# A two-layer decoder kernel: the retention's tiles placed at both ends of the on-chip memory, the experts' weights loaded inside the retention stage, and the last groups' routing written out

## The chip, the cores and the metric

The kernel runs on one core of one Trainium2 chip, as one launch. Its time is the device time in microseconds (us). A change is judged by the median of several runs: before the change, twelve runs gave a median of 1694.53 us, from 1690.32 to 1700.62. One core has a matrix engine (PE, with PEld for loading its stationary operand), a vector engine (DVE), a scalar engine (ACT), a general engine (POOL) and an engine that here only issues transfers (SP). Each takes its own instructions in order and waits on semaphores for the others.

## The reference, cut to what matters

The input x has 32 sequences of 128 tokens with 256 channels, in float32, and there is a context of the same shape. Six sublayers follow one another, each of the form x = x + f(layernorm(x), ...): in layer 0 an attention, a retention against the context, and a mixture of eight experts; in layer 1 another attention-like sublayer, a cross attention, and another mixture of experts. The change touches the border between the second and the third:

```python
def _L0_xattn_ref(query, key, value, W_Q, W_K, W_V, g_w, g_b, out_w, out_b):   # retention
    q, k, v = (einsum('bld,hde->bhle', ...) for query, key, value)             # 16 heads of 16
    q, k = _xpos(q, downscale=False), _xpos(k, downscale=True)
    sim = einsum('bhnd,bhsd->bhns', q, k) * _decay_mask(L, H)[None]
    ret = einsum('bhns,bhsd->bhnd', sim, v)
    ret = (ret - mean(ret)) / sqrt(var(ret) + GN_EPS)                          # per head
    gate = silu(query @ g_w.T + g_b)
    return ret * gate @ out_w.T + out_b

def _L0_ffn_ref(x, Wg, W1, W2, W3):                # 8 experts, D = 256, H = 512, the best 2
    top_vals, top_idx = top_k(x @ Wg, 2)
    weights = softmax(top_vals), placed at top_idx
    return sum over e of weights[e] * ((silu(x @ W1[e]) * (x @ W2[e])) @ W3[e])
```

## The kernel before, in words

**Stages.** `sublayers` calls the stages in order: `stage_a` (first attention), `stage_b` (retention), `stage_c` (the experts of layer 0), then the stages of layer 1. x stays in the on-chip memory all the time, in eight groups of GB = 4 sequences. The pools of a stage are opened when it begins and given back when it ends, so a later stage's tiles lie where an earlier stage's were, and the first write to such a tile waits for the last reader of what lay there.

**Retention.** `stage_b` loops `for b in range(B + 8)` over the 32 sequences, as a pipeline of steps written out by hand. In pass b the sequence b+2 is projected, b+1 is turned and scored, b is multiplied with its values (`values`, matmuls at L897) and normed per head (`norm`: variance on DVE, L915, inverse root on POOL, L149, product and bias on POOL), b-2 is gated (`gated`: transposes at L928, product on DVE at L930, tile b_oT) and b-3 gets its output projection (`out`: matmuls at L935, sum into x on DVE at L939). The last eight passes only drain this pipeline. The order on PE is the written one (`manual_schedule`); the instructions of DVE, ACT and POOL are ordered by the compiler's scheduler, which a hint (`order`, here as the argument `behind`) can tie to come after a given instruction.

**Routing.** When the four sequences of a group have left the retention, the group is routed to the experts, in five steps one pass apart, from pass 4g+7 on: `start` (statistics of the layer norm on DVE, L175, whose inverse root ln_rs is one POOL instruction at L149), `norm` (four DVE instructions at L203 write the normed tokens into the tile c_h), `turn` (transposes at L241, copies by ACT and DVE at L244 and L246 into c_hT), `choose` (router matmuls at L158; some twenty small DVE instructions at L320 to L341 find the best two experts, the last of them giving r_both; they also write two columns of c_h), and `place` (matmuls at L356 and L357 count the tokens ahead; DVE works out the rows r_rowi). From pass 4g+11 on, `store` writes one sequence's c_h into the table r_xs in device memory, by two indirect scatters that POOL issues (L344), one for each of the two experts chosen: eight scatters a group. Only the last group's stores stand behind the loop. The tile c_h has two buffers, so group g's norm may write only when group g-2's scatters have read theirs.

**Experts.** `stage_c` opens a pool for the experts' weights, the tile c_wx, of 12.6 MB, and loads it on SP with one transfer of 1.5 MB for each expert (L1007). Its place is where the retention's tiles lay. Then come small loads for later (`load_late`, L106), and `finish` works out where each expert's tokens begin. The table is read in 71 blocks of 128 tokens (L443, tile c_xb), each by a plain transfer on SP that must follow all scatters. On PE a block takes two transposes (L1026), eight matmuls into the two hidden halves (L1034), four transposes (L1047) and eight matmuls out (L1054); the weights are addressed by an expert number in a register, read for twelve blocks at a time. The result leaves by an indirect scatter (L344).

Of the kernel before, what the change touches and what calls it, by code (L numbers as in the profile page):

```python
# [22 lines left out]
F32 = mybir.dt.float32  # L23
# [5 lines left out]
P = 128  # L29
B = 32  # L30
# [11 lines left out]

NX = 2 * NC * FF0 + NF0 * D
# [18 lines left out]
WB = dict(q=(0, 256), k=(256, 256), v=(512, 272), kr=(784, 128), g=(912, 256), o=(1168, 256))  # L62
N_WB = 1424


class K:
# [51 lines left out]
    def load_late(self, pool):  # L118

        self.const = pool  # L120
        self.rows2 = self.load("rows2", [1, N_ROWS - N_ROWS1])
        self.wE = self.load("wE", [P, NC, 2 * D])
        self.wr1 = self.load("wr1", [P, NC, E])
        self.sw1 = self.load("sw1", [P, NC, P])
        self.sw2 = self.load("sw2", [P, D])
        self.rb2 = self.load("rb2", [P, D])
        self.eb = self.load("eb", [P, E])
# [20 lines left out]
    def rsqrt(self, out, in_, n):  # L148
        self.nc.gpsimd.tensor_tensor(out, in_, self.mhalf[: in_.shape[0], 0:n], ALU.pow)  # L149
# [344 lines left out]
class Route:  # L494
# [11 lines left out]
    def norm(self, behind=None):  # L506
        self.h = self.tile([P, GB, W["r"]], "h", bufs=2)
        self.k.normed(self.g, self.h, self.stats, behind)

    def turn(self):  # L510
        self.hT = self.tile([P, NC, GT], "hT")
        self.k.transposed(self.hT, self.h)
# [232 lines left out]
def load_b(k, p1):  # L745

    for name, key, shape in (
        ("wB", "wB", [P, NC, N_WB]), ("trig", "trig", [P, 2, 2 * D]), ("decay", "decay", [P, 4, 4, P]),
        ("ob", "outb", [P, D]),
    ):  # L750
        t = p1.tile(shape, F32, name=f"b_{name}")
        k.nc.sync.dma_start(out=t, in_=k.ins[key])
        setattr(k, name, t)


def stage_b(k, p1):
# [6 lines left out]
    with (  # L763
        tc.tile_pool(name="b2", bufs=2) as p2,
        tc.tile_pool(name="b3", bufs=3) as p3,
        tc.tile_pool(name="c2", bufs=1) as pc,
    ):
        trig, decay, ob = k.trig, k.decay, k.ob
# [19 lines left out]
        class Group:  # L788
            def __init__(self, g):
# [11 lines left out]
                self.gate = p2.tile([P, NC, GB, P], F32, name="b_gate")  # L801
# [26 lines left out]
        class Seq:  # L828
# [63 lines left out]
            def values(self):  # L892
# [9 lines left out]
                self.rT = p2.tile([P, NC, P], F32, name="b_rT")  # L902
                nc.scalar.copy(self.rT, pr)

            def norm(self):
# [3 lines left out]
                self.ret = p3.tile([P, H, HD], F32, name="b_ret")  # L909
                nc.scalar.copy(self.ret, pt.rearrange("p (h d) -> p h d", d=HD))  # L910
                sq = p2.tile([P, H, HD], F32, name="b_sq")
                nc.scalar.activation(sq, self.ret, AF.Square)
                var = p2.tile([P, H], F32, name="b_var")
                nc.vector.tensor_reduce(var, sq, AX.X, ALU.add)
                nc.vector.tensor_scalar(var, var, 1.0 / HD, GN_EPS, ALU.mult, ALU.add)  # L915
                rs = p2.tile([P, H], F32, name="b_rs")
# [7 lines left out]
            def gated(self):  # L924
# [4 lines left out]
                self.oT = p2.tile([P, NC, P], F32, name="b_oT")  # L929
                self.gated_by = nc.vector.tensor_mul(self.oT, pt, self.group.gate[:, :, self.i, :]).ins  # L930

            def out(self):
                po = k.bank([P, D])
                for c in range(NC):
                    nc.tensor.matmul(  # L935
                        po, lhsT=self.oT[:, c, :], rhs=k.wb("o", c), start=c == 0, stop=c == NC - 1
                    )
# [3 lines left out]
        with tc.manual_schedule(engines={mybir.EngineType.PE}):  # L941
# [19 lines left out]
            for b in range(B + 8):  # L961
# [31 lines left out]
                if 0 <= lag < NG - 1:  # L993
                    routes[lag].store(rest, seqs[b].last if b < B else None)
            for rest in range(GB):
                routes[NG - 1].store(rest)


def stage_c(k, later):
    nc, tc = k.nc, k.tc  # L1000
    with (
        tc.tile_pool(name="c1", bufs=1) as p1,
        tc.tile_pool(name="c3", bufs=3) as p3,
    ):
        wx = p1.tile([P, E, NX], F32, name="c_wx")
        for e in range(E):
            nc.sync.dma_start(out=wx[:, e, :], in_=k.ins["wx"][e])  # L1007
        later()
# [3 lines left out]
        def weights(j, o, n):  # L1012
            return wx[:, bass.ds(d.regs[j][0], 1), o : o + n].rearrange("p n f -> p (n f)")

        class Block:
# [15 lines left out]
            def up(self, u):  # L1031
                pu = k.bank([P, FF0], "s")
                for c in range(NC):
                    nc.tensor.matmul(  # L1034
                        pu, lhsT=self.xT[:, c, :], rhs=weights(self.j, (2 * c + u) * FF0, FF0),
# [15 lines left out]
            def down(self):  # L1051
                py = k.bank([P, D])
                for f in range(NF0):
                    nc.tensor.matmul(  # L1054
                        py, lhsT=self.hid[:, f, :], rhs=weights(self.j, 2 * NC * FF0 + f * D, D),
# [715 lines left out]
def sublayers(ctx, k):  # L1771
# [4 lines left out]
    with tc.tile_pool(name="b1", bufs=1) as pb:  # L1776
        def later():
            load_b(k, pb)
            k.empty = p1.tile([P, W["r"]], F32, name="r_empty")
            k.nc.vector.memset(k.empty, 0.0)  # L1780
            k.nc.vector.memset(k.empty[:, D : D + 2], -1.0)
            k.table("r", B, pd)
            k.deal = Deal(k, p1)
            k.disp = Dispatch(k, "r", 0, B, p1, p2)
            for n, name in enumerate(("g0", "g1")):
                k.table(name, B // 2, pd)
            for e in range(E):
                k.clear("r", e)

        stage_a(k, later)  # L1790
        stage_b(k, pb)
    late = pool("late")
    stage_c(k, lambda: k.load_late(late))
# [44 lines left out]
def layout(inputs):  # L1838
# [16 lines left out]
    def spread(w):  # L1855
# [27 lines left out]
            rep_w.reshape(D, P), a["L0_xattn_g_w"].T, a["L0_xattn_out_w"].T,  # L1883
        ], axis=1)),
        outb=np.broadcast_to(a["L0_xattn_out_b"], (P, D)),
        wg0=chunks(a["L0_ffn_Wg"]),
        wx=np.concatenate([
            w12.reshape(E, 2, NC, P, FF0).transpose(0, 3, 2, 1, 4).reshape(E, P, -1),
            a["L0_ffn_W3"].reshape(E, NF0, P, D).transpose(0, 2, 1, 3).reshape(E, P, -1),
        ], axis=2),  # L1890
# [36 lines left out]
```

## Time and profile before

| what | value |
|---|---|
| median of 12 runs | 1694.53 us |
| profiled execution | 1700.53 us |
| its span, from first to last instruction | 1698.4 us |
| mean PE clock granted | 0.921 |
| busy time: PE, PEld | 1488.4 (88%), 986.1 (58%) |
| busy time: DVE, ACT, POOL | 930.1 (55%), 606.1 (36%), 602.0 (35%) |
| r_xs scatters of L344 on POOL | 64, in all 64.3 us |
| ln_rs of L149 on POOL | 40, in all 40.7 us, 1022 ns each |
| c_wx loads | 8, of 1536 KB each |
| chain by engine | PE 69%, DVE 12%, POOL 5%, issue 5%, ACT 5%, DMA 3% |

By stretch, from a table of windows (us of the span; busy us of PE, DVE and POOL; granted clock; DMA share):

| window | what runs | PE | DVE | POOL | clock | DMA |
|---|---|---|---|---|---|---|
| 282 to 540 | most of the retention | 241.07 | 189.80 | 183.70 | 0.99 | 0.26 |
| 540 to 604 | its end, routing of groups 5 to 7, load of the weights | 22.62 | 30.99 | 37.43 | 0.59 | 0.69 |
| 604 to 1024 | the experts of layer 0 | 417.40 | 141.72 | 68.33 | 0.99 | 0.15 |

How to read such a profile: a busy share is a mean over stages with different limits, so a stage is read by itself. A row of a timeline gives the start, the length, the engine, the line, the operation, the tiles written and read, their shapes, and in square brackets how long the engine stood idle before it and what released it. A chain of waits goes back from an instruction to whatever released it, step by step; where a DMA stands in it, its length is the time from issue to landing. "issue" means that nothing the profile shows was waited for. An idle engine costs time only where the chain passes through it.

### The profile page before, as it was taken

Reading aid. Unit: us, or ns where it says so; the run is one execution under the profiler, and the core shown is the slowest. Engines: PE = TensorE matmul, PEld = TensorE weight load, DVE = VectorE, ACT = ScalarE, POOL = GpSimd, SP = SyncE. Lnnn points to the kernel's source line nnn. Section 1 sums busy time; section 2 is a strip of 40 time slices with the busy share of each in tenths; the row PEclk is TensorE's granted clock in tenths of the full one; section 3 lists DMA queues with packets and bytes.
Section 4 is the critical chain, followed back from the end, with each engine's and each line's share of the span. In section 5 each row is a group of like instructions: output and inputs, shape, how many; then the busy total and the mean of one; then the engine's idle time right before and its main releaser. Section 6 shows DMA issues by size and latency. Waiting matters only on the chain.

```text
span 1698.4 us, 26941 instructions
## 1 busy us (share of the span) xinstructions
PE 1488.4 (88%) x9233; PEld 986.1 (58%) x9233; DVE 930.1 (55%) x3005; ACT 606.1 (36%) x1542; POOL 602.0 (35%) x621
## 2 busy tenths in 40 slices
PE   6999799999998379999999994789999998878882
PEld 4555567776776346666666664445555554456672
DVE  6666446777778533333333324546567766554565
ACT  2444333433333022222222221155665554433341
POOL 2111136577768511111111113121233433365553
PEclk8999999999999589999999995799999998778997
DMA  9990199711000821111111108000000110043486
GB/s 337 336 336 18 54 326 318 228 39 36 24 26 33 349 95 49 44 45 48 47 45 44 50 23 314 13 6 6 3 2 14 53 55 26 26 128 110 131 269 228
DMA packets 133113, 183.85 MB, mean 108 GB/s; under 512 B 12043, under 2 KB 113237, under 8 KB 130933
## 3 DMA queue, kind: packets, MB, share of 16 engines
q1 hardware_dynamic: 116356, 142.28, 26.8%
q0 software_dynamic: 13296, 36.52, 6.0%
q10 hardware_dynamic: 3328, 3.33, 0.6%
q8 instruction: 77, 1.26, 0.3%
q14 instruction: 56, 0.45, 0.1%
HBM read 69.80 MB, written 112.30 MB: 107 GB/s over the span
## 4 chain that ended last, share of the span: by engine, by line
PE 69%; DVE 12%; POOL 5%; issue 5%; ACT 5%; DMA 3%; another core or an unknown queue 1%; POOLq 0%; ACTq 0%; SPq 0%; DVEq 0%
PE ps L1034 13%; PE ps L1054 6%; PE ps L158 5%; PE ps L666 3%; PE ps L1458 3%; PE ps L1418 2%; PE ps L1436 2%; PE ps L1642 2%; PE ps L1658 2%; PE ps L241 2%; PE ps L881 2%; PE ps L1047 2%; PE ps L153 2%; PE ps L897 1%; PE ps L840 1%
## 5 line engine op out<-in xcount | busy, mean ns | idle before, releaser
L1034 PE MATMUL ps<-c_wx,c_xT 128*128 x568 | 268.8, 596 | 0.0
L344 POOL DMA_INDIRECT r_ys<-c_yb,r_toi x71 | 67.9, 956 | 356.0 <-DVE r_w L462 315.7
L1034 PEld LDWEIGHTS ps<-c_wx,c_xT 128*128 128x128 f32 x568 | 103.2, 192 | 73.8 <-issue 70.3
L1054 PE MATMUL ps<-c_wx,c_hid 128*128 x568 | 134.8, 380 | 0.9 <-DVE c_hid L1049 0.9
L1054 PEld LDWEIGHTS ps<-c_wx,c_hid 128*128 128x128 f32 x568 | 107.4, 190 | 47.2 <-issue 17.9
L887 DVE TENSOR_TENSOR b_sim<-ps,b_decay 128x512 f32<-128x512 f32 x128 | 79.5, 682 | 84.5 <-PE ps L881 51.2
L149 POOL TENSOR_TENSOR b_rs<-b_var,mhalf 128x16 f32<-128x16 f32 x32 | 93.6, 2927 | 82.8 <-DVE b_var L915 79.7
L1059 ACT ACTIVATE c_yb<-ps,r_w 128x256 f32<-128x256 f32 x71 | 33.7, 474 | 219.2 <-PE ps L1054 219.2
L1049 DVE COPY c_hid<-ps 128x512 f32<-128x512 f32 x71 | 49.1, 691 | 101.2 <-PE ps L1047 101.2
L344 POOL DMA_INDIRECT g_ys<-f_yb,g_toi x78 | 75.6, 969 | 66.2 <-DVE g_to L449 49.7
L1443 DVE TENSOR_REDUCE e_pad<-ps 128x4 f32<-128x512 f32 x128 | 82.3, 681 | 13.7 <-PE ps L1436 8.9
L149 POOL TENSOR_TENSOR ln_rs<-ln_ve,mhalf 128x4 f32<-128x4 f32 x40 | 40.7, 1022 | 132.2 <-DVE ln_ve L177 132.1
L1488 POOL TENSOR_TENSOR x<-x,e_t 128x256 f32<-128x256 f32 x32 | 23.3, 727 | 163.2 <-DVE e_t L1483 163.2
L175 DVE BATCH_NORM_STATS2 ln_st<-x 128x6 f32<-128x256 f32 x192 | 74.9, 406 | 9.8 <-DMA x<-in_x_dram 5.1
L1042 DVE TENSOR_TENSOR c_su<-ps,c_su 128x512 f32<-128x512 f32 x71 | 49.1, 691 | 56.0 <-PE ps L1034 56.0
L1459 ACT ACTIVATE e_e<-ps 128x512 f32<-128x512 f32 x128 | 67.5, 605 | 28.4 <-PE ps L1458 28.2
L344 POOL DMA_INDIRECT r_xs<-c_h,r_rowi x64 | 64.3, 1004 | 28.7 <-issue 14.8
L1040 ACT ACTIVATE c_su<-ps 128x512 f32<-128x512 f32 x71 | 42.4, 597 | 86.8 <-PE ps L1034 86.8
L344 POOL DMA_INDIRECT g_xs<-f_h,g_rowi x64 | 63.2, 987 | 24.7 <-issue 15.9
L1436 PE MATMUL ps<-kp,e_qT 32*128 32x128 f32 x1024 | 67.0, 308 | 1.6 <-ACT e_e L1459 1.0
L1658 PE MATMUL ps<-f_rw,f_hb 128*128 x156 | 51.6, 415 | 15.6 <-ACT f_hb L1654 12.0
L1642 PE MATMUL ps<-f_rw,f_xT 128*128 x312 | 53.6, 299 | 11.9 <-ACT f_xT L1634 8.5
(385 smaller groups left out, 3325.2 us busy)
## 6 DMA issues: line engine op xcount, KB each, us to landing
g_xs<-r_empty SPq DMA_DIRECT2D x16, 2193.0 KB
r_xs<-r_empty SPq DMA_DIRECT2D x8, 4290.0 KB
c_wx<-in_wx_dram SPq DMA_DIRECT2D x8, 1536.0 KB
f_xb<-g_xs SPq DMA_DIRECT2D x78, 129.0 KB
c_xb<-r_xs SPq DMA_DIRECT2D x71, 130.0 KB
c_yg<-r_ys SPq DMA_DIRECT2D x8, 1024.0 KB
f_yg<-g_ys SPq DMA_DIRECT2D x16, 512.0 KB
x<-in_x_dram SPq DMA_DIRECT2D x8, 512.0 KB
```

What stands on the lines that cost most here:

```text
L149: self.nc.gpsimd.tensor_tensor(out, in_, self.mhalf[: in_.shape[0], 0:n], ALU.pow)
L158: self.nc.tensor.matmul(out, lhsT=(xT[c] if isinstance(xT, tuple) else xT[:, c])[:, i * P : (i + 1) * P], rhs=w(c), start=c == 0, stop=c = ...
L175: self.order(nc.vector.bn_stats(st[:, i, :], x[:, i, :]).ins, behind)
L344: inst = self.nc.gpsimd.indirect_dma_start(out=table, out_offset=bass.IndirectOffsetOnAxis(ap=rows, axis=0), in_=src, in_offset=None,).ins
L887: nc.vector.tensor_mul(self.sim[:, r].rearrange("p c s t -> p (c s t)"), ps[r].rearrange("p c s t -> p (c s t)"), decay[:, r].rearrange("p ...
L1034: nc.tensor.matmul(pu, lhsT=self.xT[:, c, :], rhs=weights(self.j, (2 * c + u) * FF0, FF0), start=c == 0, stop=c == NC - 1,)
L1054: nc.tensor.matmul(py, lhsT=self.hid[:, f, :], rhs=weights(self.j, 2 * NC * FF0 + f * D, D), start=f == 0, stop=f == NF0 - 1,)
L1436: nc.tensor.matmul(ps[r][:, j, :], lhsT=self.group.qT[rows, j, self.i, :], rhs=self.keys[rows, :], start=True, stop=True,)
L1443: nc.vector.tensor_reduce(slots[:, :, r, HD], ps[r], AX.X, ALU.max, negate=True)
L1459: self.exp_by = nc.scalar.activation(self.e[:, r], ps, AF.Exp, scale=1.0 / 16.0).ins
L1642: nc.tensor.matmul(pu, lhsT=self.xT[:, c, :], rhs=experts.rw1[:, self.at, c, :].rearrange("p n f -> p (n f)"), start=c == 0, stop=c == NC - 1,
L1658: nc.tensor.matmul(po, lhsT=self.hid, rhs=experts.rw2[:, self.at, :].rearrange("p n f -> p (n f)"), start=True, stop=True,)
```

## The change

The computation is the same; five things differ.

1. *Pools.* The pools of the retention that are still needed after the last `values` (b3, now with the tiles b_gate, b_rT, b_sq, b_var, b_rs, b_ret and b_oT, and c2 with the routing's tiles) lie at the right end of the memory. The output projection's weights leave the common weight tile and become a tile of their own, `wo`, in a pool bl at the right end too, with a load of their own. The pools b1 (projection weights, tables, padded values) and b2 stay at the left and are given back inside the stage, after the loop.
2. *The loop* ends at `range(B)`. Then b2 and b1 are closed and `over()` loads the experts' weights: so the load stands, on SP, ahead of the last steps, and it waits for the last readers of what lay there. After it the last steps are written out one by one: the last `gated` and `out`, and the routing of groups 5, 6 and 7. Group 6's norm has no `behind`; group 6's stores are tied behind the inverse root of group 7's layer norm (`last = k.rooted`).
3. *Buffers.* c_h has three buffers for two; c_hT comes out of the pool and the buffers of the layer norms' h.
4. *The experts' weights* are eight tiles for one: four of [128, 8, 512] for the hidden halves (2 MB each) and four of [128, 8, 256] for the output (1 MB each), loaded by eight transfers; the arrays passed to the kernel are laid out accordingly.
5. *The late loads* go to a pool at the right end.

```diff
@@ rsqrt
-        self.nc.gpsimd.tensor_tensor(out, in_, self.mhalf[: in_.shape[0], 0:n], ALU.pow)
+        inst = self.nc.gpsimd.tensor_tensor(out, in_, self.mhalf[: in_.shape[0], 0:n], ALU.pow)
+        self.rooted = inst.ins
@@ class Route
-        self.h = self.tile([P, GB, W["r"]], "h", bufs=2)
+        self.h = self.tile([P, GB, W["r"]], "h", bufs=3)
...
-        self.hT = self.tile([P, NC, GT], "hT")
+        self.hT = self.k.lnp.tile([P, NC, GT], F32, name="c_hT", tag="h")
@@ load_b
+def load_b(k, p1, last):
+    for pool, name, key, shape in (
+        (p1, "wB", "wB", [P, NC, N_WB]), (p1, "trig", "trig", [P, 2, 2 * D]), (p1, "decay", "decay", [P, 4, 4, P]),
+        (last, "wo", "wo", [P, NC, D]), (last, "ob", "outb", [P, D]),
     ):
@@ stage_b
-        tc.tile_pool(name="b2", bufs=2) as p2,
-        tc.tile_pool(name="b3", bufs=3) as p3,
-        tc.tile_pool(name="c2", bufs=1) as pc,
+        tc.tile_pool(name="b3", bufs=2, side="right") as p3,
+        tc.tile_pool(name="c2", bufs=1, side="right") as pc,
+        ExitStack() as most,
     ):
+        p2 = most.enter_context(tc.tile_pool(name="b2", bufs=2))
...
-                        po, lhsT=self.oT[:, c, :], rhs=k.wb("o", c), start=c == 0, stop=c == NC - 1
+                        po, lhsT=self.oT[:, c, :], rhs=k.wo[:, c, :], start=c == 0, stop=c == NC - 1
...
-            for b in range(B + 8):
+            for b in range(B):
...
-                if 0 <= lag < NG - 1:
-                    routes[lag].store(rest, seqs[b].last if b < B else None)
+                if 0 <= lag:
+                    routes[lag].store(rest, seqs[b].last)
+            most.close()
+            over()
+
+            r5, r6 = routes[NG - 3], routes[NG - 2]
+            step("gated", B - 2)
+            step("out", B - 3)
+            r6.norm()
+            for rest in range(1, GB):
+                r5.store(rest)
+            step("out", B - 2)
+            r6.turn()
+            step("gated", B - 1)
+            r6.choose()
+            step("out", B - 1)
+            r7 = RouteC(k, NG - 1, k.disp, pc)
+            last = k.rooted
+            r7.norm()
+            r6.place()
             for rest in range(GB):
-                routes[NG - 1].store(rest)
+                r6.store(rest, last)
+            r7.turn()
+            r7.choose()
+            r7.place()
+            for rest in range(GB):
+                r7.store(rest)
@@ experts
+class Glu:
+    def load(self, pool):
+        tile = lambda name, n: pool.tile([P, E, n], F32, name=f"c_{name}")
+        self.up = [tile(f"up{i}", FF0) for i in range(2 * NC)]
+        self.down = [tile(f"down{i}", D) for i in range(NF0)]
+        for tiles, name in ((self.up, "wxu"), (self.down, "wxd")):
+            for i, t in enumerate(tiles):
+                self.k.nc.sync.dma_start(out=t, in_=self.k.ins[name][i])
...
-        wx = p1.tile([P, E, NX], F32, name="c_wx")
-        for e in range(E):
-            nc.sync.dma_start(out=wx[:, e, :], in_=k.ins["wx"][e])
-        later()
+        k.load_late()
...
-        def weights(j, o, n):
-            return wx[:, bass.ds(d.regs[j][0], 1), o : o + n].rearrange("p n f -> p (n f)")
+        def weights(j, tile):
+            return tile[:, bass.ds(d.regs[j][0], 1), :].rearrange("p n f -> p (n f)")
@@ sublayers
+    last, most, weights = (ctx.enter_context(ExitStack()) for _ in range(3))
+    pb = most.enter_context(tc.tile_pool(name="b1", bufs=1))
+    pl = last.enter_context(tc.tile_pool(name="bl", bufs=1, side="right"))
+    glu = Glu(k)
...
+    def over():
+
+        most.close()
+        glu.load(weights.enter_context(tc.tile_pool(name="c1", bufs=1)))
+
+    stage_a(k, later)
+    stage_b(k, pb, pl, over)
+    last.close()
+    k.const = pool("late", side="right")
+    stage_c(k, glu)
+    weights.close()
```

## The prediction

> **What bounds the kernel now.** I read, in this order, the page's slices (PE falls to 3 tenths in the fourteenth slice, 552 to 594 us, while DMA stands at 8), then a table of ten-microsecond windows around that slice, the chain of waits through it, the DMA queue's own waits, and POOL's timeline. The kernel is PE-bound on both sides of the slice (PE 9 tenths or more), so what counts is the stretch from the last retention matmul to the first expert matmul.
>
> The windows (busy us of PE, PEld, DVE, ACT, POOL; PE clock; DMA share; GB/s):
>
> ```profile
> 540.00:550.00 10.00, 6.07 (x63) 5.23 (x63) 8.05 (x39) 2.65 (x5) 8.58 (x8) 0.89 0.16 55
> 550.00:560.00 10.00, 7.88 (x36) 6.44 (x34) 4.76 (x18) 0.59 (x1) 8.53 (x8) 0.60 0.15 50
> 560.00:570.00 10.00, 0.43 (x4) 0.33 (x3) 2.51 (x18) 0.21 (x1) 4.39 (x5) 0.57 0.98 387
> 590.00:600.00 10.00, 0.00 (x0) 0.00 (x0) 3.68 (x10) 0.00 (x0) 6.31 (x7) 0.50 0.98 386
> ```
>
> PE does almost nothing from 560 to 604 us, the DMA engines are full from 560 to 600, and PE's clock sinks to 0.5. It looks as if the weights' load were the wait. The chain says otherwise (start, us, what):
>
> ```profile
> 563.29 8.34 DMA r_xs<-c_h,r_rowi
> 571.76 0.41 DVE c_h L203
> ...
> 597.18 4.40 DMA r_xs<-c_h,r_rowi
> 601.78 0.35 SPq L443
> 602.32 2.32 DMA c_xb<-r_xs
> ```
>
> The reader is to see that two landings of routing scatters carry it: the last scatter of group 5 lands 8.34 us after its issue and only then may the norm of group 7 overwrite that buffer; and the last scatter of group 7 lands at 601.58, after which the first block is read and PE starts at 603.95. The load of the weights itself (line 1007) is seen in the queue's waits:
>
> ```profile
> SPq L1007 <- DVE b_oT L930: 169.9, 1, 169.9
> SPq L1007 <- PE ps L935: 4.0, 1, 4.0
> SPq L106 <- DMA c_wx<-in_wx_dram: 22.5, 6, 4.6
> ```
>
> It is issued at 558.87, when the last L935 is done. The small loads behind it (L106) each wait for one weight load; the seventh is done at 592.59, and at 22.5 / 6, some 4 us each, the eighth at about 597. That is 4.6 us before the scatter's 601.58: the load is not the last wait, though it slows those that are. POOL's queue in between:
>
> ```profile
> 541.81 2.94 POOL L149 TENSOR_TENSOR b_rs<-b_var,mhalf 128x16 f32<-128x16 f32 x1 [0.70 <-DVE b_var L915]
> ...
> 546.34 1.06 POOL L344 DMA_INDIRECT r_xs<-c_h,r_rowi  x1 [0.17 <-issue]
> 547.70 0.96 POOL L344 DMA_INDIRECT r_xs<-c_h,r_rowi  x1 [0.30 <-issue]
> 548.68 1.04 POOL L149 TENSOR_TENSOR ln_rs<-ln_ve,mhalf 128x4 f32<-128x4 f32 x1
> ...
> 554.33 1.06 POOL L344 DMA_INDIRECT r_xs<-c_h,r_rowi  x1 [0.17 <-issue]
> ...
> 563.29 0.96 POOL L344 DMA_INDIRECT r_xs<-c_h,r_rowi  x1 [0.30 <-issue]
> 564.26 1.05 POOL L149 TENSOR_TENSOR ln_rs<-ln_ve,mhalf 128x4 f32<-128x4 f32 x1
> ```
>
> A group's eight scatters take 554.33 to 564.25, 1.27 us each, and group 6's ln_rs, at 548.68, stands behind two of them.
>
> **The change, part by part.** The order of the built kernels shows the same instructions on PE, DVE, ACT and POOL, moved only in the tail, and one DMA more on SP. Times below are on the clock of the profiled execution.
>
> *The load moves.* Its first DMA now waits for the last L897, which ends at 541.54 + 1.08 = 542.62, not for L935 at 558.74: 16.1 us earlier, at about 542.75. The old load took from 558.87 to 597, 38 us; so it ends near 581. Alone this gains nothing on the chain, since a scatter was 4.6 us later than it; it takes the load away from the end, where the scatters of group 7 land. With busy DMA the last landing took 4.40; at the end of the expert stage, with idle DMA, the same kind of scatter took 2.95 (1023.56 to 1026.51). I take 2.95: minus 1.45.
>
> *Third buffer for c_h.* Group 7's norm now waits for scatters issued at 546.34 and 547.70, long landed, not for the one at 563.29. In the old run ln_rs was ready at 565.31 and the norm began at 571.76: 6.45 us of wait go. What is late next is ln_rs itself.
>
> *The new order on DVE.* This costs. Without its ordering hint, the norm of group 6 (L203) now stands right behind r_m of 544.15, ahead of the var of the last sequence and of all of group 5's choosing. It needs ln_rs, which POOL ends at 549.72 as before. So DVE stands still from 544.33 to 549.8. Behind it: PE's place matmuls (L356) of group 5, behind them on PE the last gated and out steps; b_var for POOL's last b_rs. From 549.8 I add pitches of the old timeline (0.33 for each 256-wide operation, 0.1 to 0.2 for each small one): four L203, var, two L939 and L175, and the small ones make 3.75, so r_both is issued at 553.55 where it was 547.72; L356 at 553.85 (548.07), L357 ends near 555.1, r_at 555.15, and the rows, behind b_oT, at 556.7 (550.8). Group 5's eight scatters run from 556.85, not 554.33: 2.5 later, to 566.75. One thing can lengthen this: L915 took 0.70 beside a POOL operation and 0.16 without; a small DVE operation caught so beside POOL's b_ret and x (0.62 + 0.72) costs up to 1.4. I take none, and keep 1.4.
>
> *PE meanwhile.* Idle since 544.64, it resumes at half clock: L928 0.67 and L935 1.91 to 557.65, as at 549.03. In the old run four microseconds of work brought the full clock back (L241 1.91 from 555.72, then L158 x16 in 1.85 from 558.58). So from 557.9: L935 to 558.9, L241 x8 1.04 to 559.9, c_hT 0.7, L158 1.85 to 562.5, L935 1.03 to 563.5; then DVE's choose steps and the last statistics to about 565.2. That is before POOL is free at 566.75, so POOL decides: ln_rs to 567.8, the norm of group 7 at 567.85. It was 571.76: minus 3.9.
>
> *From there* to the next matmul (L241, 574.85 before) the old run took 3.09; in the new order r_both stands before the third L203, and I count 2.75: minus 0.35. Then nothing differs up to POOL's first scatter of group 7 (587.84 before), and PE is again at half clock, having idled 5 us (2.6 us sufficed at 531.7). Sum at that point 4.25 earlier, 583.6; group 6's scatters, from 571.8, are out by 581.7. The last scatter follows 8.9 later (7 x 1.27; 9.34 before): minus 0.45. Then the landing, minus 1.45, and 2.37 as before to PE.
>
> *The sum:* -3.9 -0.35 -0.45 -1.45 = -6.15; I round to -6.0. The profiled execution took 1700.53 (span 1698.4 and 2.1 around it), 6.0 above the median of the runs, 1694.53. It would take 1694.5, and the median 1688.5.
>
> *At nothing:* the weights as eight tiles of 2 and 1 MB for eight of 1.5 MB (same bytes; in the expert stage each block takes PE 5.82 us with no gap, so addresses are computed under it); the output weights as a load of their own (one issue, 0.43 on SP, behind it table clears whose queue then waits 90.8 us for DVE; without that cover 0.43); c_hT in the norms' buffers; the late loads, now free after the last L935 and done well before 590.
>
> *A rule against it.* The Trainium skill, "DMA: Bandwidth & Descriptors", section "Queues, rings and completion order", has each DMA engine go round its queues and empty a whole packet of one before the next. In the trace four scatters issued from 559.50 to 563.29 had landed by 571.63, with the load in flight from 560.9: 2.7 each, faster than one per weight load of 4.4. By the rule, with larger tiles, one scatter per load, estimated at 5.9 us for a 2 MB tile and 3 for a 1 MB one: group 5's eighth lands at 581.5 and holds back group 6's eighth, which waits for it. The sum would be -5.3. By the trace's 2.7 it lands at 578.5, before that scatter's turn at 580.7, and the sum stays.
>
> **The rivals.**
> *Half clock to the end of the retention (chance 0.17).* If PE does not regain its clock at 557.9, L935, L241, L158 and L935 take 1.9, 1.95, 3.2 and 1.9, the statistics end at 568.8 and the norm starts at 570.05: 2.2 given back, 1690.7. With the DVE lock's 1.4 on top, 1692.1. For it: L158 still took 3.17 at 577.58 after 3 us of work with gaps. Against: 558.58.
> *Full clock for group 7's steps too (0.12).* L241, L158 and the place matmuls would save 0.9, 1.3 and 0.3: 1686.0. Against: every gap over 2.5 us in this trace was followed by slow matmuls.
> *The scatters starve, slower (0.06).* Place: POOL's scatter of group 6 waits for the one eight before it. If group 5's land only when the load ends, at 581.5, group 6's first starts at 582.6, group 7's last at 601.7, PE at 607.0: 3.1 later than 603.95, 1697.6. It decides from the point where group 5's first lands later than 579.5, 22.7 us after its issue; the longest landing in the chain is 8.34.
> *The change gains nothing (0.05).* If the norm of group 7 waited past 571.8 for anything, only the 1.45 and 0.45 would remain, less the DVE lock: 1694.
>
> **How the numbers follow.** The worked sum holds 0.60. A difference under 0.2% (3.4 us) can't be told from none here; 1691.1 is the bound. Faster: 0.60 + 0.12 + about half of the first rival, 0.80. Same: the rest of it, the last rival and part of the starving, 0.15. Slower 0.05. The range 1685.0 to 1693.0 takes in both clock rivals with the DVE lock and leaves out the last two.
>
> **What would show it.** Right: the first weight load issued near 542.8; DVE idle until 549.8, released by POOL's ln_rs; L356 near 553.9; the norm of group 7 near 567.9, released by ln_rs and no longer by a landing; a last landing near 3 us; PE's first expert transpose near 598. Wrong: a DVE stall that is not there or much longer, POOL waiting between scatters, slow L158 before 563, or a last landing of over 4 us.

## The result, and the profile after

The changed kernel takes 1687.26 us (median of 12 runs, 1684.93 to 1691.40). The kernel before, run beside it, takes 1695.9; the ratio (of the means) is 0.9953, with a 95% interval from 0.9939 to 0.9966. That is 8.0 us less, between 5.8 and 10.3. The forecast was 1688.5, 6.0 less, within 1685.0 to 1693.0.

The profiled execution has a span of 1684.2 against 1698.4, but only half of these 14.2 us lie in the stretch that the change is about. The last matmul of the retention (L897) ends at 537.59 for 542.62, so 5.0 us were won ahead of that stretch. They go with the granted clock: the same DVE instructions come 2.1 us earlier after the first of the two windows below (first stage) and 5.2 earlier after the second (the retention's start), and little changes between or behind them (us; busy us of PE, PEld, DVE, ACT, POOL; clock; DMA share; GB/s). Before:

```profile
0.00:50.00 50.00, 35.59 (x113) 21.30 (x114) 36.10 (x124) 15.73 (x62) 11.12 (x33) 0.90 1.03 337
200.00:250.00 50.00, 42.53 (x341) 31.33 (x342) 19.16 (x39) 16.38 (x44) 11.60 (x8) 0.90 0.97 290
```

After:

```profile
0.00:50.00 50.00, 35.79 (x121) 20.74 (x122) 38.24 (x129) 17.53 (x71) 11.11 (x33) 0.97 1.04 336
200.00:250.00 50.00, 43.10 (x386) 31.77 (x384) 21.94 (x47) 17.33 (x46) 14.71 (x11) 0.97 1.02 299
```

In a second pair of traces, described below, L897 ends at 540.08 before and at 539.73 after: that difference comes and goes. So in all that follows times are counted from the end of the last L897. From there to the first expert matmul the kernel before took 61.33 and the changed one takes 54.23, 7.1 less. From there to the end of the span it is 1094.45 and 1092.38.

The windows of the changed kernel around that stretch, with the same columns:

```profile
540.00:550.00 10.00, 1.50 (x7) 1.50 (x8) 5.02 (x29) 0.94 (x2) 8.23 (x8) 0.64 1.00 423
560.00:570.00 10.00, 5.70 (x25) 5.28 (x25) 4.15 (x22) 0.58 (x1) 5.01 (x6) 0.50 1.01 414
570.00:580.00 10.00, 2.54 (x11) 2.22 (x10) 7.06 (x46) 0.20 (x1) 6.43 (x7) 0.50 0.84 326
580.00:590.00 10.00, 0.00 (x0) 0.00 (x0) 4.02 (x11) 0.00 (x0) 6.05 (x7) 0.50 0.26 93
```

The DMA engines are full from 540, where they were from 560 before; they are quiet when the last scatters land. In the waits of SP's queue the first weight load (now L1034) has waited for the last L897 and for no output projection:

```profile
SPq L1034 <- DVE b_sim L887: 156.3, 1, 156.3
SPq L1034 <- PE ps L897: 1.6, 1, 1.6
SPq L104 <- DMA c_down<-in_wxd_dram: 6.2, 2, 3.2
```

The chain (start, us, what; lines stand two lower than before, so L201 is the norm, L239 the transposes, L342 the scatter, and the experts' L1058, L1066 and L1086 were L1026, L1034 and L1054):

```profile
561.33 1.06 POOL ln_rs L146
562.42 0.41 DVE c_h L201
...
565.18 1.77 PE ps L239 x8
...
585.65 2.54 DMA r_xs<-c_h,r_rowi
588.23 1.13 issue
589.54 2.14 DMA c_xb<-r_xs
591.82 1.21 PE ps L1058 x4
```

The norm of group 7 is released by ln_rs; the landing of 8.34 us has left the chain, and the last landing is short.

The second trace of the changed kernel needs a closer look here. Its chain names a landing ahead of this norm (first two lines), but that landing is done at 564.17, while ln_rs ends at 563.49 + 1.05 = 564.54 (third line, POOL's timeline), and the norm starts 0.04 us after that. There too ln_rs came last.

```profile
556.18 7.99 DMA r_xs<-c_h,r_rowi
564.17 0.41 issue
563.49 1.05 POOL L146 TENSOR_TENSOR ln_rs<-ln_ve,mhalf 128x4 f32<-128x4 f32 x1
```

### The profile page after: what moved, and what is told of

It reads as the page before. It is cut to its first block, busy times and chain, and to the rows that moved or that the text cites. A ratio compares the mean times of both kernels' runs of the same rounds, so it can differ in the third digit from the quotient of the medians.

```text
span 1684.2 us, 26942 instructions
## 1 busy us (share of the span) xinstructions
PE 1487.4 (88%) x9233; PEld 985.2 (58%) x9233; DVE 928.6 (55%) x3005; ACT 605.2 (36%) x1542; POOL 602.7 (36%) x621
## 4 chain that ended last, share of the span: by engine, by line
PE 72%; DVE 11%; issue 5%; ACT 5%; POOL 5%; DMA 1%; another core or an unknown queue 1%; POOLq 0%; ACTq 0%; DVEq 0%; SPq 0%
PE ps L1066 13%; PE ps L1086 7%; PE ps L156 6%; PE ps L664 3%; PE ps L1490 3%; PE ps L1468 2%; PE ps L1450 2%; PE ps L1674 2%; PE ps L1690 2%; PE ps L881 2%; PE ps L151 2%; PE ps L239 2%; PE ps L1079 2%; PE ps L897 2%; PE ps L840 1%
## 5 line engine op out<-in xcount | busy, mean ns | idle before, releaser
L1066 PE MATMUL ps<-c_up,c_xT 128*128 x568 | 269.0, 597 | 0.0
L342 POOL DMA_INDIRECT r_ys<-c_yb,r_toi x71 | 68.1, 959 | 354.1 <-DVE r_w L460 313.8
L1066 PEld LDWEIGHTS ps<-c_up,c_xT 128*128 128x128 f32 x568 | 103.2, 192 | 74.2 <-issue 69.7
L1086 PE MATMUL ps<-c_down,c_hid 128*128 x568 | 134.8, 380 | 0.9 <-DVE c_hid L1081 0.9
L1086 PEld LDWEIGHTS ps<-c_down,c_hid 128*128 128x128 f32 x568 | 107.4, 190 | 47.2 <-issue 17.9
L342 POOL DMA_INDIRECT g_ys<-f_yb,g_toi x78 | 75.4, 966 | 68.0 <-DVE g_to L447 51.9
L342 POOL DMA_INDIRECT r_xs<-c_h,r_rowi x64 | 63.7, 996 | 23.0 <-issue 13.7
L342 POOL DMA_INDIRECT g_xs<-f_h,g_rowi x64 | 62.7, 980 | 20.8 <-issue 16.4
```

What stands on the lines that cost most here:

```text
L342: inst = self.nc.gpsimd.indirect_dma_start(out=table, out_offset=bass.IndirectOffsetOnAxis(ap=rows, axis=0), in_=src, in_offset=None,).ins
L1066: nc.tensor.matmul(pu, lhsT=self.xT[:, c, :], rhs=weights(self.j, glu.up[2 * c + u]), start=c == 0, stop=c == NC - 1,)
L1086: nc.tensor.matmul(py, lhsT=self.hid[:, f, :], rhs=weights(self.j, glu.down[f]), start=f == 0, stop=f == NF0 - 1,)
```

## The experiments

**Theory.** Two things must come together: group 7's norm must not wait for a landing (third buffer), and the weights' load must be away from the end. Either alone gains little, since the other is late next. **Rival A:** the early load is what pays. **Rival B:** the buffer is what pays.

The runs fall on three chips: number 9 (the buffers and the load), 11 (the hints one by one and the first added matmuls) and 14 (the repeats and the last two runs). The kernel before took 1653 to 1654 us on the first two and 1694 on the third (1695.9 in the first measurement, whose chip isn't on record), so only ratios, and times from the end of L897, are compared. Positions (us from the end of L897):

| kernel | norm of group 6 | norm of group 7 | last scatter | first read of c_xb | first block on PE | ratio to before, interval |
|---|---|---|---|---|---|---|
| before | 7.64 | 29.14 | 54.56 | 59.16 | 61.33 | |
| before, again | 7.44 | 29.05 | 53.75 | 59.69 | 61.90 | |
| changed | 7.09 | 24.83 | 49.33 | 51.95 | 54.23 | 0.9953, 0.9939 to 0.9966 |
| changed, again | 7.10 | 24.85 | 49.72 | 52.34 | 54.42 | 0.9957, 0.9940 to 0.9974 |
| changed, two buffers | 13.85 | 34.62 | 58.04 | 60.67 | 62.93 | 1.0004, 0.9984 to 1.0024 |
| before, three buffers | 7.93 | 23.34 | 48.38 | 57.85 | 60.06 | 0.9996, 0.9976 to 1.0016 |
| changed, load late | 7.85 | 25.58 | 49.82 | 60.99 | 63.85 | 0.9992, 0.9974 to 1.0010 |
| load alone | 13.74 | 31.13 | 55.34 | 58.17 | 60.36 | 0.9998, 0.9979 to 1.0017 |

Up to its added matmuls the run that keeps the clock up (below) is the changed kernel on chip 11: norm of group 6 at 7.85, of group 7 at 25.59, last scatter at 49.85, first read of c_xb at 52.58. So positions of one kernel differ by up to 0.8 us from chip to chip.

### The repeats

The changed kernel and the one before, each as it was, on chip 14.

> The changed kernel once more, on the same chip as the other runs of this call, so that the stretch from the last L897 to the first block can be compared on one chip. Theory: ratio to before 0.995 again, first block 54.2 to 54.8 us behind the last L897 (54.23 in the first trace). Rival (the first measurement was lucky or bound to its chip): ratio above 0.997.

> The kernel before once more, for its trace on this chip. Theory: the first block comes 61.3 to 61.9 us behind the last L897, as in its first trace (61.33), though the whole time may differ by some per cent from chip to chip. Rival: the stretch itself changes with the chip by over 1 us, and then the differences between runs of different chips must be read again.

The ratio is 0.9957 and the stretch 54.42 against 61.90, 7.5 less. Two traces of each kernel agree within 0.9 us (the last scatter of the kernel before, 54.56 and 53.75, differs most).

### The third buffer taken back

```diff
-        self.h = self.tile([P, GB, W["r"]], "h", bufs=3)
+        self.h = self.tile([P, GB, W["r"]], "h", bufs=2)
```

> The changed kernel with c_h back at two buffers; all else as changed, the early load and the written-out routing too. Theory (the gain comes from group 7's norm no longer waiting for the landing of group 5's last scatter): the norm waits again. That scatter is issued at 560.35 in the trace of after, with the load still under way; if it lands after 8.34 us as before the change, the norm starts at 568.7 for 562.42, everything behind it is 6.3 later, and the time is about 1693.5, 0.37% over after; if it lands as fast as scatters do without a load (2.95) it is 563.3 and the time 1688. Rival (what paid is that the weights are there early): the load still starts near 538 and ends near 575, so the time stays at 1687.3, ratio to before 0.995.

The whole gain is gone, and rival A falls. In the trace it is dearer than expected (first block at 62.93, where 6.3 us more would have been 60.5), by a wait that I had not seen. From the chain of this run:

```profile
540.95 7.88 DMA r_xs<-c_h,r_rowi
...
562.73 6.87 DMA r_xs<-c_h,r_rowi
...
593.15 2.43 DMA r_xs<-c_h,r_rowi
595.78 2.13 DMA c_xb<-r_xs
```

The second landing is the one expected: group 5's last scatter, before group 7's norm. The first is group 4's, before group 6's norm, which starts at 13.85 for 7.09. Before the change that landing was over in time; with the load in flight it takes 7.88. So the early load makes the third buffer necessary twice.

### The load alone

The changed kernel with two buffers and with the old order on DVE:

```diff
-        self.h = self.tile([P, GB, W["r"]], "h", bufs=3)
+        self.h = self.tile([P, GB, W["r"]], "h", bufs=2)
...
-            r6.norm()
+            r6.norm(seqs[B - 2].gated_by)
```

> The load alone: the changed kernel with c_h at two buffers and with group 6's norm ordered behind the gated product of sequence 30, as in the kernel before, so that the routing runs in the old order. Theory: the norm of group 7 waits for the landing as before; only the last landing is faster (4.4 before, 2.5 in the trace of after): 2 less than before, 1694, ratio 0.9988. Rival (the load was what PE waited for): 1688 or less, ratio 0.995.

No change that can be measured; the stretch is 1.0 to 1.5 shorter than in the two traces of before. The norm of group 6 pays 6 us for the landing of group 4's scatter (13.74 for 7.64), which reaches group 7's norm as 2.0; the landings at the end give it back.

### The third buffer alone

The kernel before, with `bufs=3` for c_h.

> The kernel before with a third buffer for c_h and nothing else. Theory: the norm of group 7 starts at 565.3 for 571.8 and the last scatter is issued 6.4 earlier, near 590.8; but the weights' load, which still starts at 558.9 and ends near 597, is then the last wait, so that PE starts near 599.5 for 603.95: 4.4 less, 1691.5, ratio 0.9974. The first read of c_xb would be released by a weight load. Rival A (only the routing decides): 6.4 less, 1689.5, ratio 0.9962. Rival B (only the load decides): no change, ratio 1.000.

The norm comes where it was expected (23.34), but the ratio is 0.9996: rival B falls too. The first read of c_xb moves by 1.3 us where the last scatter moved by 6.2. What holds it is not quite what the theory said. The end of the chain of this run:

```profile
580.56 0.96 POOL r_xs L344
581.82 9.27 DMA r_xs<-c_h,r_rowi
591.29 2.07 DMA c_xb<-r_xs
```

The last scatter needs 9.27 us to land, since the load is in full flight (4.40 and 5.74 in the two traces of before, 2.4 to 2.6 in those with the early load). The load takes the gain by slowing the landing until it is itself done.

### The load late

The changed kernel with the output weights' tile at the left end, under the first weight tile, and the load behind the last output projection:

```diff
-        (p1, "wB", "wB", [P, NC, N_WB]), (p1, "trig", "trig", [P, 2, 2 * D]), (p1, "decay", "decay", [P, 4, 4, P]),
-        (last, "wo", "wo", [P, NC, D]), (last, "ob", "outb", [P, D]),
+        (p1, "wo", "wo", [P, NC, D]), (p1, "wB", "wB", [P, NC, N_WB]), (p1, "trig", "trig", [P, 2, 2 * D]),
+        (p1, "decay", "decay", [P, 4, 4, P]), (last, "ob", "outb", [P, D]),
...
-            most.close()
-            over()
...
             step("out", B - 1)
+            most.close()
+            over()
```

> The changed kernel, with the load of the weights back behind the last output projection: the tile of the output weights lies at the left end, where the first weight tile goes, so the first load waits for the last L935 (557.7 in the trace of after). Third buffer and written-out routing stay. Theory: the load, 37.5 us as in both traces, ends near 595.2, and the first read of c_xb waits for it: PE starts near 597.5 for 591.8, time 1693.0, ratio to before 0.998. Rival (the load is off the path and only slows the last landing by 1.5 to 2): 1689, ratio 0.996.

The end of its chain:

```profile
555.56 35.85 DMA c_down<-in_wxd_dram
591.55 2.73 DMA c_xb<-r_xs
```

A weight load now releases the first read, as the theory said; the last scatter had been issued 11 us earlier. PE starts 9.6 later than in the changed kernel, not 5.7: the load took 40.0 us (20.86 to 60.85) where I had 37.5, started 0.7 later than I had it, and the read behind it took longer. The ratio, 0.9992, is again no change.

### One ordering hint: the norm of group 6

The changed kernel with the old order on DVE, three buffers and the early load.

```diff
-            r6.norm()
+            r6.norm(seqs[B - 2].gated_by)
```

> The changed kernel with one ordering hint: group 6's norm stands on DVE behind the gated product of sequence 30, as it did before the change. Theory (the DVE stall on ln_rs costs): DVE no longer stands still from 539.3 to 544.7 in front of L201; group 5's first scatter comes as soon as POOL has done the last b_ret and x, 4.6 us behind ln_rs for 6.75, so 2.1 earlier, and all behind it too: 1685.2, 0.12% under after, ratio to before about 0.994. Rival (the stall is hidden, since POOL or PE is the later one): 1687.3, as after.

The stall on DVE is gone (0.30 us ahead of the norm of group 6, where it was 5.38):

```profile
541.42 0.41 DVE L201 TENSOR_SCALAR c_h<-x,ln_mv,ln_rs 128x256 f32<-128x256 f32 x1 [0.30 <-POOL ln_rs L146]
```

The norm of group 7 starts at 23.34 for 24.83, and PE's first block comes at 51.95. The ratio is 0.9931 (0.9908 to 0.9954); its interval overlaps that of the changed kernel, so the gain of the hint rests on the positions. This run is also the fourth corner beside the load alone and the third buffer alone, since it has both and the old order on DVE: each alone starts the first block at 60.4 and 60.1, both together at 51.95.

### And the norm of group 7 behind group 6's choosing

```diff
-            r7.norm()
+            r7.norm(k.disp.counted)      # the last r_cum of the group chosen before
```

> As the run before, and group 7's norm on DVE is ordered behind group 6's choosing. In the trace of after r_both of group 6 (L336) stands behind the first L201 of group 7, which waits 2.25 us for ln_rs; PE's place matmuls of group 6 wait for it, and group 7's transposes (L239, 564.99) wait on PE behind those. Theory: the four L201 come in a row, L239 0.1 behind them: 1.2 less than the run before, 1684.0. Rival: nothing, since POOL's scatters of group 6 now set the start of group 7's: 1685.2.

The last scatter is issued at 45.12 for 47.02, 1.9 earlier (1.2 expected); the first block at 49.91. The ratio, 0.9923 (0.9897 to 0.9950), can't be told from that of the run before. POOL's timeline still shows a pause ahead of group 6's first scatter, because its rows now stand behind group 7's norm on DVE:

```profile
555.30 1.05 POOL L146 TENSOR_TENSOR ln_rs<-ln_ve,mhalf 128x4 f32<-128x4 f32 x1
558.81 1.04 POOL L342 DMA_INDIRECT r_xs<-c_h,r_rowi  x1 [2.46 <-DVE r_m L361]
```

### And the count of blocks behind group 7's rows

```diff
-        nc.vector.tensor_copy(count, pn)
+        inst = nc.vector.tensor_copy(count, pn).ins
+        self.k.order(inst, self.placed if self.name == "r" else None)
```

> As the run before, and the count of blocks (finish, L380 to L420) is ordered on DVE behind group 7's rows. In the trace of after seven of its instructions stand between r_at at 575.34 and the second r_rowi at 578.19, 2.85 us, where group 6 takes 2.36 and group 5 2.99, and the first scatter waits until 578.06. Theory: the first scatter of group 7 comes 0.7 earlier: 1683.3. Rival: finish itself, which ended at 584.16, comes 1 us later and takes nothing, but the gap on DVE at 577 has another cause: as the run before.

A miss: 0.3 at the first scatter of group 7 and 0.1 at the first block, ratio 0.9931 (0.9903 to 0.9959). Group 7's rows were ready earlier, but POOL's sixteen scatters now follow one another at 1.27 us from 557.60 to 577.6, with a pause of no more than 0.32: POOL has become the last.

### Matmuls to keep the clock up

The changed kernel with matmuls whose results nobody reads, between the end of `finish` and the first block:

```diff
+        if self.name == "r":
+            pw = self.k.bank([P, 2, D])
+            nc.tensor.matmul(pw[:, 0, 0:nblk], lhsT=self.k.ident, rhs=br, start=True, stop=True)
+            for _ in range(12):
+                nc.tensor.matmul(pw, lhsT=self.k.ident, rhs=self.k.x[0][:, 0:2, :], start=True, stop=True)
```

> The changed kernel with 13 matmuls more on PE, whose results nobody reads, between the end of finish (584.16) and the first block (591.82), so that PE is busy in that gap. It prices the half clock at the start of the expert stage: there the first twelve L1066 took 7.56 us, 0.63 each, where later four take 1.72, 0.43 each. Theory (after some 4 us of work the granted clock is full): L1058 and the twelve L1066 take 2.6 less: 1684.7. Rival A (13 matmuls do not last to 591.8 or do not bring the clock back): 1687.3. Rival B (they last longer than the gap, at half clock 0.87 each for 10.7 us in all, to 594.9): 1 to 3 more than after, less the 2.6.

From PE's timeline of this run (lines are 5 higher than in the changed kernel):

```profile
580.32 12.04 PE L426 MATMUL ps<-x,ident 128*128 128x512 f32 x24
592.19 0.60 PE L1063 MATMUL ps<-ident,c_xb 128*128 128x128 f32 x4
593.16 5.42 PE L1071 MATMUL ps<-c_up,c_xT 128*128 x12 [0.36 <-ACT c_xT L1065]
```

and of the changed kernel:

```profile
591.82 1.21 PE L1058 MATMUL ps<-ident,c_xb 128*128 128x128 f32 x4 [16.13 <-DMA c_xb<-r_xs]
593.06 7.56 PE L1066 MATMUL ps<-c_up,c_xT 128*128 x12
```

I had counted a matmul as one record, but it makes two: 24 records took 12.04, past the gap, and delayed the first block by about 4 (58.67 against 54.42). Behind them it took 6.39 from the first transpose to the end of the twelve L1066 (592.19 to 598.58), for 8.80 in the changed kernel (591.82 to 600.62): 2.4 is the price of the half clock there. In the other runs without added matmuls ahead of that block the same stretch took 7.65 to 9.28, so the price ranges from 1.3 to 2.9. Net nothing: 0.9951 (0.9931 to 0.9971).

### All of it

The three hints, group 6's rows ahead of group 7's norm, and six matmuls instead of thirteen.

```diff
-            r7.norm(k.disp.counted)
-            r6.place()
+            r6.place()
+            r7.norm(k.disp.placed)
...
-            for _ in range(12):
+            for _ in range(5):
```

> The three ordering hints of the run with the late finish, group 6's rows (L357 to L365) also ahead of group 7's norm on DVE, and six matmuls (no result read) on PE between the end of finish and the first block. In that earlier run POOL went through the sixteen scatters of groups 6 and 7 with no pause, group 6's first 2.46 us behind ln_rs because its rows stood behind L201. Theory: group 6's scatters start right behind ln_rs, 2.4 earlier, and then group 7's rows, not POOL, hold group 7's first scatter: 0.3 earlier. The six matmuls (23 more records of half a matmul took 12 us in the first warm-up, 11 take about 6.5) end before the first block, and the first twelve L1066 take 5.4 for 6.5 to 8.0: 1 to 2.6 less. Together 1.3 to 2.9 under the run with the late finish: ratio to before about 0.991. Rival: the clock falls again before the first block or does not rise, and POOL's order gives nothing: 0.993.

Two rows of POOL's timeline, the first scatters of groups 6 and 7:

```profile
562.20 1.04 POOL L342 DMA_INDIRECT r_xs<-c_h,r_rowi  x1 [0.20 <-issue]
...
575.03 0.96 POOL L342 DMA_INDIRECT r_xs<-c_h,r_rowi  x1 [2.88 <-DVE r_m L361]
```

PE's timeline around the first block:

```profile
582.86 6.00 PE L427 MATMUL ps<-x,ident 128*128 128x512 f32 x10
588.70 0.39 PE L1064 MATMUL ps<-ident,c_xb 128*128 128x128 f32 x2
589.59 0.44 PE L1064 MATMUL ps<-ident,c_xb 128*128 128x128 f32 x2 [0.51 <-DMA c_xb<-r_xs]
589.87 5.32 PE L1072 MATMUL ps<-c_up,c_xT 128*128 x12
```

Group 6's scatters follow ln_rs at once, and those of group 7 wait for their rows. The added matmuls end just before the first block, and the first twelve L1066 take 5.32. The first block is at 49.33, and the first matmul of the experts' second layer (c_hid), which holds the clock's gain too, at 58.03, for 65.46 in the changed kernel beside it. The ratio is 0.9907 (0.9886 to 0.9928), 1679.48 us against 1686.91 for the changed kernel on the same chip and 1694.19 for the one before: it beats both.

### And matmuls ahead of group 7's transposes

```diff
             r6.place()
+            pw = k.bank([P, 2, D])
+            for _ in range(3):
+                nc.tensor.matmul(pw, lhsT=k.ident, rhs=k.x[0][:, 0:2, :], start=True, stop=True)
             r7.norm(k.disp.placed)
```

> As the run before, with three matmuls more (no result read) on PE between group 6's place matmuls and group 7's transposes, where PE stood idle for 4.5 us. Theory: at full clock group 7's L239 take 1.04 for 2.2 and its L156 1.73 for 3.15, so its rows come 2.5 earlier; POOL, through with group 6's scatters 2.3 us before group 7's first in the run before, lets 2.2 of it through: 2.2 less, ratio to before about 0.9895. Rival A: the three matmuls hold up L239 and the clock does not rise: as the run before or up to 1 us more. Rival B: POOL's scatters are in a row anyway: no gain.

PE's timeline of this run:

```profile
561.78 5.47 PE L1020 MATMUL ps<-x,ident 128*128 128x512 f32 x6
567.04 1.23 PE L239 MATMUL ps<-ident,c_h 128*128 128x128 f32 x8
...
569.06 1.73 PE L156 MATMUL ps<-w_wg,c_hT 128*128 128x8 f32 x14 [0.16 <-issue]
575.19 0.61 PE L354 MATMUL ps<-r_both,r_tri 128*128 128x32 f32 x2 [4.41 <-DVE r_sel L324]
```

Group 7's steps ran at full clock as expected, and L156 ended 2.7 earlier (27.0 for 29.7 from L897). But only 0.7 of it reached the scatters (34.92 for 35.66): 1.2 went between the end of L156 and DVE's copy of it, and the rest in DVE's choosing. I have no explanation for that; it stays open. Nor is the 0.7 shown to come from the added matmuls: already ahead of them the steps came earlier than in the run before (group 6's first scatter 22.24 for 22.83, group 7's norm 22.08 for 22.96). At the end the second lot of matmuls ran some 0.9 past the arrival of the first block, since ten records took 6.89 here and 6.00 above. The ratio is 0.9910 (0.9890 to 0.9929): no difference from the run before.

## Why the prediction was right

Its steps against the trace of after, in us from the end of the last L897:

| step | before | predicted | after |
|---|---|---|---|
| first weight load issued | 16.25 | 0.13 | 0.16 |
| r_both of group 5 (DVE) | 5.10 | 10.93 | 10.58 |
| first scatter of group 5 | 11.71 | 14.23 | 13.81 |
| norm of group 7 | 29.14 | 25.23 | 24.83 |
| transposes of group 7 | 32.23 | 27.98 | 27.40 |
| first scatter of group 7 | 45.22 | 40.98 | 40.47 |
| last scatter | 54.56 | 49.88 | 49.33 |
| first block on PE | 61.33 | 55.20 | 54.23 |

*The stall on DVE* was there as described: the timeline of DVE shows it, and again a shorter one ahead of group 7's norm, which the prediction did not name.

```profile
544.68 0.41 DVE L201 TENSOR_SCALAR c_h<-x,ln_mv,ln_rs 128x256 f32<-128x256 f32 x1 [5.38 <-POOL ln_rs L146]
...
562.42 0.41 DVE L201 TENSOR_SCALAR c_h<-x,ln_mv,ln_rs 128x256 f32<-128x256 f32 x1 [2.25 <-POOL ln_rs L146]
```

The extra 1.4 of a blocked small DVE operation did not occur: L915 took 0.17. The stall moved group 5's first scatter by 2.1 (13.81 for 11.71), where the sum had 2.5; the hint that removes it gave 2.3 at the first block (51.95 for 54.23).

*The norm of group 7* starts 4.3 earlier, by the sum 3.9, since the stall cost 0.4 less; from it to the transposes 0.5 (0.35); the eight last scatters 0.48 (0.45).

*The clock* did as the sum had it, not as its two rivals: after 4 us of work at half clock the last retention steps ran at full clock, and group 7's steps at half, as PE's timeline shows:

```profile
549.92 3.44 PE L935 MATMUL ps<-b_wo,b_oT 128*128 128x256 f32 x8
553.19 1.04 PE L239 MATMUL ps<-ident,c_h 128*128 128x128 f32 x8
...
564.99 1.95 PE L239 MATMUL ps<-ident,c_h 128*128 128x128 f32 x8
```

*The last term was too small.* From the last scatter to PE it took 4.90 for 6.77, 1.87 less where the sum had 1.45: the landing needs 2.4 to 2.6 on idle queues, not the 2.95 that I took from the end of the expert stage. In all the sum had -6.15 and the trace shows -7.1 and, in the second pair, -7.5; the ratios say -8.0 and -7.3. The steps were right, and what was mis-sized (the stall, the steps from the norm to the transposes, the last landing) lay on the same side.

*"Alone this gains nothing"*, said of the load, is borne out (0.9998), but the working behind it was incomplete. It counted what the load costs at its old place and not what it costs at its new one: landings of 7 to 8 us for the scatters of groups 4 and 5. The third buffer hides both, so the forecast was not hurt.

*At nothing*: the split tiles and the separate output weights show no cost. From the first matmul of the experts' second layer to the end of the span it is 1081.3 and 1079.4 in the two traces of after, 1083.6 and 1082.2 before. Why it is 2 to 3 us less isn't shown; the last run above, on the same chip as the second pair, has 1073.0 there, so single executions differ by more than that.

*The rule against it.* The Trainium skill, "DMA: Bandwidth & Descriptors", section "Queues, rings and completion order", has engines change queues a packet at a time. That a scatter then waits for a whole load was my reading of it; by that reading, in the order of the prediction, group 5's eighth scatter would have landed some 16 us after its issue (an estimate: 581.5 for an issue near 565.7). It landed 6.87 us after its issue with two buffers and 7.45 in the run of the load alone, while SP's queue was already waiting for the 1 MB tiles (c_down), the last of the load; the runs are against that reading. Nor did larger tiles visibly slow a scatter: early in the load, where the 2 MB tiles are, group 4's last one landed after 7.88 and 7.78 in these two runs; beside loads of 1.5 MB, landings of 7.11 and 9.27 are in the chain of the third buffer alone.

*How long the half clock lasts.* In the first run with added matmuls the 24 records took 12.04 us, about 20 at 0.43 and 4 at twice that; with the two records ahead of them PE worked 3.5 us at half clock (granted clock 0.50 until 583.3, 1.00 from 583.5). The Trainium skill, "TensorE: Matmul & The Clock Gate", section "Part 1: The HAM clock gate (the "warmup" mystery)", names about 3.4 us of sustained work, and adds that the count varies from run to run. The ten records at 6.00 (four slow) agree. In the last run the half clock lasted longer than that figure: 5.1 us of work for the ten records at 6.89 (granted clock 0.50 from 586.06 to 591.2), and 6.4 us ahead of group 7's transposes (0.50 from 560.82 to 567.2), where all six records were slow.

*What brings the half clock.* The prediction took from its trace that a pause of 2.6 us on PE suffices. The same pause ahead of the same L865 was not followed by it in the run with two buffers (granted clock 1.00 until 540); the trace of before, then that run:

```profile
534.23 1.11 PE L865 MATMUL ps<-ident,b_qk 128*128 128x128 f32 x4 [2.57 <-POOL b_qk L854]
528.16 0.66 PE L865 MATMUL ps<-ident,b_qk 128*128 128x128 f32 x4 [2.58 <-POOL b_qk L854]
```

So this premise was no rule. The forecast did not suffer: the two pauses that it applied this to were longer (8.89 and 5.86 us in the trace of after), and half clock followed both.

## What to carry to other kernels

Moving a large load out of a wait moves its contention too: look for every small transfer that will now be in flight with it, and for the buffer that waits on that transfer's landing (here 7 to 9 us for 2.4 to 2.6). Where two waits end within a few us of each other, cost them together: the load alone and the buffer alone gave nothing that could be measured, and both together gave 0.45%, or 0.69% with the old order on DVE. When steps are written out by hand, keep or replace each ordering hint, since an instruction that waits holds everything queued behind it (DVE stood still for 5.38 us here); by the positions, the hints on DVE brought some 4.5 us more.

## What the runs showed that I had not expected

- The same scatter lands 2.4 to 2.6 us after its issue when the DMA engines are nearly idle and 6.9 to 9.3 when a load of 1 to 2 MB tiles fills them (share 1.00 in the windows).
- A pause on PE and the half clock behind it need not be cause and effect. In the last run L354 took 0.61 after a pause of 2.41 us, but the granted clock stood at 0.50 from 557.2, before that pause began: four matmuls of L941 ahead of it took 1.65 us, where 1.11 is usual (row below). After a pause of 3.13 us in the same run the clock stayed at 1.00 for another 1.4 us of work and then fell (0.50 from 550.4).

```profile
556.76 1.65 PE L941 MATMUL ps<-b_wo,b_oT 128*128 128x256 f32 x4
```

- The kernel before took 1653 to 1654 us on chips 9 and 11 and 1694 on chip 14, so the time goes with the chip, as far as three can show; what differs in them is open. Most of the difference lies in the last stage, where the DMA share from 1500 to 1630 was 0.49 in the first trace of the changed kernel and 0.67 in the first hint's (chip 11): in the former its blocks (f_xb) run from 1488.8 to 1651.4, 163 us, and in the latter from 1480.6 to 1607.8, 127 us.
